# Item stage of a recommendation kernel: part of the gathered neighbours read by ScalarE, VectorE and SyncE instead of GpSimd

## The chip, the cores and the metric

The kernel runs on one core of a Trainium2 chip. The metric is device microseconds (us) of one execution. The time before is 36,303.63 us, the median of three runs that lie between 36,298.54 and 36,312.89 us. The profile is one further execution, and its own time is given below beside its span.

Engine names follow the profile: PE is TensorE, DVE is VectorE, ACT is ScalarE, POOL is GpSimd, SP is SyncE. PEld is the loading of weights into PE. SPq, ACTq and POOLq are the queues in which those engines issue DMAs.

## The reference

Every item has a row of 32 numbers in each of two tables, `E_in` and `E_out`, and a list of 32 neighbour items. For every item and both tables the reference takes a softmax attention over the item's neighbours; the result is used for 16,384 users with 100 history items each.

```
def _neighbor_attn(E, near_full):                  # twice: E_in and E_out, 50001 x 32
    V = E[near_full]                               # 50001 x 32 neighbours x 32
    scores = einsum('nd,nkd->nk', E, V) / sqrt(32)
    w = softmax(scores, axis=-1)
    return einsum('nk,nkd->nd', w, V)
...
h = concat([E_hist[history], a_sus[history], a_inf[history]])   # 16384 x 100 x 128
t = concat([E_tgt[target], a_inf[target], a_sus[target]])       # 16384 x 128
x = h * t[:, None, :]
z = relu(x @ W1.T + b1)
scores = z @ W2[0]                                 # then a masked exponential weighting, and a
...                                                # cosine and sigmoid for each user
```

All values are float32. The item numbers are random, so neighbour rows lie anywhere in the tables.

## The kernel before

The work has two stages, one after the other. They meet in two tables in DRAM, `table` and `ttab`, which the first stage writes and the second gathers from.

**The item stage** (lines 94 to 164) goes over 50,048 items (`ROWS`, the items with padding) in 23 iterations of 17 tiles (`NITER`, `NSUB`). A tile is 128 items, one on each partition; there are 391. `egeo` in DRAM holds both tables side by side, so one item's row is 64 floats, 256 bytes. At the start of an iteration SP loads the neighbour numbers `nidx`, the items' own rows `own`, and 64 columns of `row`. Then, for each tile:

- POOL gathers: 32 indirect DMAs (line 111), each of which fetches for all 128 items the row of their k-th neighbour into `v`, a tile of 128 x 32 x 64. `v` has five buffers, so POOL can be five tiles ahead of the arithmetic.
- ACT copies the items' own rows into PSUM (line 118).
- DVE multiplies all neighbours with the own row (`prod`, line 120), sums to scores (`sc`, line 127), takes the maximum and scales it (`top`, lines 129 and 130).
- ACT takes the exponentials with their sum (`ex`, `tot`, line 134).
- DVE inverts the sum (line 142), weighs the neighbours (`wv`, line 145, one instruction for each of the two tables), sums (`att`, line 152) and writes into `row` (line 153).
- ACT copies two halves, exchanged, into `trow` (line 160).

After 17 tiles SP writes `row` and `trow` to the tables (lines 163 and 164). The pools and the framework's scheduler set the order on each engine; a tile's instructions all stand before the next tile's. PE does nothing in this stage.

**The user stage** (lines 166 to 276) is not touched. For 128 groups of 128 users it gathers 100 history rows each with POOL (line 233), turns them on PE, multiplies by the target row, and runs the two matrix products.

The `with` statement that opens the item stage's pools, and the loops inside it, are what the diff replaces.

Of the kernel before, what the change touches and what calls it, by code (L numbers as in the profile page):

```python
# [9 lines left out]

F32 = mybir.dt.float32
I32 = mybir.dt.int32
AF = mybir.ActivationFunctionType
ALU = mybir.AluOpType
AX = mybir.AxisListType

P = 128
ITEMS = 50001
K = 32
G = 32  # L20
DE = 64
D = 128
# [7 lines left out]
NSUB = 17  # L30
NITER = -(-ITEMS // (P * NSUB))
ROWS = NITER * P * NSUB

# [7 lines left out]
def kernel(  # L43
# [11 lines left out]
    out: bass.AP,  # L55
):
    nc = tc.nc

    const = ctx.enter_context(tc.tile_pool(name="const", bufs=1))
    dram = ctx.enter_context(tc.tile_pool(name="dram", bufs=1, space=bass.MemoryType.DRAM))  # L60


    table = dram.tile([ROWS, D], F32, name="table")

    ttab = dram.tile([ROWS, D], F32, name="ttab")

    ident = const.tile([P, P], F32, name="ident")
# [16 lines left out]
    scale = 1.0 / math.sqrt(G)  # L84
    near_v = near.rearrange("(i p j) k -> i p j k", p=P, j=NSUB)
    egeo_v = egeo.rearrange("(i p j) d -> i p j d", p=P, j=NSUB)
    ehist_v = ehist.rearrange("(i p j) d -> i p j d", p=P, j=NSUB)
    table_v = table.rearrange("(i p j) d -> i p j d", p=P, j=NSUB)
    ttab_v = ttab.rearrange("(i p j) d -> i p j d", p=P, j=NSUB)

    nc.scalar.dma_start(ttab[0 : ITEMS - 1, 0:DE], etgt[0 : ITEMS - 1, :])
    nc.scalar.dma_start(ttab[ITEMS - 1 : ITEMS, 0:DE], etgt[ITEMS - 1 : ITEMS, :])
    with (
        tc.tile_pool(name="n_in", bufs=2) as n_in,
        tc.tile_pool(name="n_v", bufs=5) as n_v,
        tc.tile_pool(name="n_p", bufs=2) as n_p,
        tc.tile_pool(name="n_s", bufs=3) as n_s,
        tc.tile_pool(name="n_ps", bufs=2, space=bass.MemoryType.PSUM) as n_ps,
    ):
        for it in range(NITER):  # L100
            nidx = n_in.tile([P, NSUB, K], I32, name="nidx")
            nc.sync.dma_start(nidx, near_v[it])
            own = n_in.tile([P, NSUB, 2 * G], F32, name="own")
            nc.sync.dma_start(own, egeo_v[it])
            row = n_in.tile([P, NSUB, D], F32, name="row")
            nc.sync.dma_start(row[:, :, 0:DE], ehist_v[it])
            trow = n_in.tile([P, NSUB, 2 * G], F32, name="trow")
            for j in range(NSUB):
                v = n_v.tile([P, K, 2, G], F32, name="v")
                for k in range(K):  # L110
                    nc.gpsimd.indirect_dma_start(  # L111
                        out=v[:, k].rearrange("p t d -> p (t d)"),
                        out_offset=None,
                        in_=egeo,
                        in_offset=bass.IndirectOffsetOnAxis(ap=nidx[:, j, k : k + 1], axis=0),
                    )
                own_ps = n_ps.tile([P, 1, 2 * G], F32, name="own_ps")
                nc.scalar.copy(own_ps[:, 0, :], own[:, j, :])  # L118
                prod = n_p.tile([P, K, 2, G], F32, name="prod")
                nc.vector.tensor_tensor(  # L120
                    prod.rearrange("p k t d -> p k (t d)"),
                    v.rearrange("p k t d -> p k (t d)"),
                    own_ps.to_broadcast([P, K, 2 * G]),
                    ALU.mult,
                )
                sc = n_s.tile([P, 2, K], F32, name="sc")
                nc.vector.tensor_reduce(sc.rearrange("p t k -> p k t"), prod, AX.X, ALU.add)  # L127
                top = n_s.tile([P, 2], F32, name="top")
                nc.vector.tensor_reduce(top, sc, AX.X, ALU.max)
                nc.vector.tensor_scalar(top, top, -scale, None, ALU.mult)  # L130
                ex = n_ps.tile([P, 2, K], F32, name="ex")
                tot = n_s.tile([P, 2, 1], F32, name="tot")
                for t in range(2):
                    nc.scalar.activation(  # L134
                        ex[:, t, :],
                        sc[:, t, :],
                        AF.Exp,
                        bias=top[:, t : t + 1],
                        scale=scale,
                        accum_out=tot[:, t, :],  # L140
                    )
                nc.vector.reciprocal(tot, tot)  # L142
                wv = n_p.tile([P, 2, G, K], F32, name="wv")
                for t in range(2):
                    nc.vector.tensor_tensor(  # L145
                        wv[:, t].rearrange("p d k -> p k d"),
                        v[:, :, t, :],
                        ex[:, t, :].rearrange("p (k o) -> p k o", o=1).to_broadcast([P, K, G]),
                        ALU.mult,
                    )  # L150
                att = n_s.tile([P, 2, G], F32, name="att")
                nc.vector.tensor_reduce(att, wv, AX.X, ALU.add)  # L152
                nc.vector.tensor_tensor(  # L153
                    row[:, j, DE:D].rearrange("p (t d) -> p t d", t=2),
                    att,
                    tot.to_broadcast([P, 2, G]),
                    ALU.mult,
                )
                for t in range(2):
                    nc.scalar.copy(  # L160
                        trow[:, j, t * G : (t + 1) * G], row[:, j, D - (t + 1) * G : D - t * G]
                    )
            nc.sync.dma_start(table_v[it], row)
            nc.sync.dma_start(ttab_v[it][:, :, DE:D], trow)


    num = const.tile([P, UC], F32, name="num")
# [3 lines left out]
    hist_v = history.rearrange("(p i j) l -> i p j l", p=P, j=BSUB)  # L171
    tidx = const.tile([P, UC], I32, name="tidx")
    nc.scalar.dma_start(tidx, target.rearrange("(p c) -> p c", p=P))
    tidf = const.tile([P, UC], F32, name="tidf")
    nc.vector.tensor_copy(tidf, tidx)
    with (
# [12 lines left out]
        def target_rows(c):  # L189

            if c % BSUB == 0:
                hidx = u_in.tile([P, BSUB, L], I32, name="hidx")
                nc.sync.dma_start(hidx, hist_v[c // BSUB])
# [11 lines left out]
        def target_work(c):  # L205
# [8 lines left out]
            junk = u_t.tile([P, D], F32, name="junk")  # L214
            nc.scalar.activation(junk, t, AF.Square, accum_out=tsq[:, c : c + 1])
            idf = u_s.tile([P, L], F32, name="idf")
# [11 lines left out]
        def gather(c, g):  # L228
            u = users[c]
            h = u_h.tile([P, LG, D], F32, name="h")  # L230
            for q in range(LG):
                l = g * LG + q
                nc.gpsimd.indirect_dma_start(  # L233
                    out=h[:, q, :],
                    out_offset=None,
                    in_=table,
                    in_offset=bass.IndirectOffsetOnAxis(ap=u["hidx"][:, l : l + 1], axis=0),
                )
            u["h", g] = h

        def turn(c, g):
            u = users[c]
            h = u.pop(("h", g))
            hT_ps = ps_t.tile([P, LG, P], F32, name="hT_ps")
            for q in range(LG):
                nc.tensor.transpose(hT_ps[:, q, :], h[:, q, :], ident)  # L246
            xT = u_x.tile([D, LG, P], F32, name="xT")
            nc.vector.tensor_tensor(xT, hT_ps, u["tT"].to_broadcast([D, LG, P]), ALU.mult)  # L248
            nc.vector.tensor_reduce(u["hsum"][:, g * LG : (g + 1) * LG], h, AX.X, ALU.add)  # L249
            u["xT"][g] = xT  # L250

        def hidden(c, g):
# [3 lines left out]
            z = u_x.tile([HID, LG, P], F32, name="z")  # L256
            nc.scalar.activation(z, z_ps, AF.Relu, bias=b1_sb)  # L257
            u["z"][g] = z

        def scored(c, g):  # L260
# [9 lines left out]
            ea = u_s.tile([P, L], F32, name="ea")  # L270
            nc.scalar.activation(ea, u["score"], AF.Exp)
            nc.vector.tensor_tensor(ea, ea, u["keep"], ALU.mult)
# [7 lines left out]
        for s in range(len(groups) + 2):  # L280
            if s < len(groups):
                c, g = groups[s]
# [12 lines left out]
    with (  # L295
# [3 lines left out]
        root = f_s.tile([P, UC], F32, name="root")  # L299
        nc.scalar.activation(root, den, AF.Sqrt)  # L300
        part = f_s.tile([P, UC], F32, name="part")
# [6 lines left out]
        s = f_s.tile([P, 1], F32, name="s")  # L308
# [4 lines left out]
        nc.vector.tensor_scalar(n1, n1, float(D), EPS * EPS, ALU.mult, ALU.max)  # L313
        nc.scalar.activation(n1, n1, AF.Sqrt)
        n2 = f_s.tile([P, UC], F32, name="n2")
# [65 lines left out]
```

## Time and profile before

| | |
|---|---|
| median of three runs | 36,303.63 us |
| the profiled execution, whole | 31,810.23 us |
| its span, first to last instruction | 31,808.5 us |
| first and last gather issue of the item stage (line 111) | 9.7 and 15,626.3 us |
| first gather issue of the user stage (line 197) | 15,649.06 us |
| HBM read and written | 1,308.76 MB and 51.30 MB |
| SP's DMAs in the whole kernel | 151 |

The profiled execution is 14% shorter than the runs that were timed. Durations and stage times are from the profile, and they are compared with the span. The page gives busy time by engine, the span in 40 slices, the DMA queues, the chain of work that ended last, and the costliest groups of instructions. In a group's row, the busy time and the mean duration of one instruction stand after the first bar, and after the second the idle time of the engine just before such instructions, with what ended it. "issue" there means that the engine waited for nothing that the profile shows.

### The profile page before, as it was taken

Reading aid. Unit: us, or ns where it says so; the run is one execution under the profiler, and the core shown is the slowest. Engines: PE = TensorE matmul, PEld = TensorE weight load, DVE = VectorE, ACT = ScalarE, POOL = GpSimd, SP = SyncE. Lnnn points to the kernel's source line nnn. Section 1 sums busy time; section 2 is a strip of 40 time slices with the busy share of each in tenths; the row PEclk is TensorE's granted clock in tenths of the full one; section 3 lists DMA queues with packets and bytes.
Section 4 is the critical chain, followed back from the end, with each engine's and each line's share of the span. In section 5 each row is a group of like instructions: output and inputs, shape, how many; then the busy total and the mean of one; then the engine's idle time right before and its main releaser. Section 6 shows DMA issues by size and latency. Waiting matters only on the chain.

```text
span 31808.5 us, 154035 instructions
## 1 busy us (share of the span) xinstructions
PE 15238.9 (48%) x44931; PEld 9632.2 (30%) x44931; DVE 8951.2 (28%) x10957; ACT 2851.2 (9%) x6458; POOL 24005.7 (75%) x25446
## 2 busy tenths in 40 slices
PE   0000000000000000000299999999999999999999
PEld 0000000000000000000155555555555555555555
DVE  2222222222222222222222222222222222222222
ACT  0000000000000000000011111111111111111111
POOL 7777777777777777777777777777777777777777
PEclk9999999999999999999955555555555555555555
DMA  2111111111111111111122222222222222222221
GB/s 50 30 30 30 30 31 33 30 30 30 30 34 30 30 30 30 31 33 28 37 54 53 54 53 54 53 54 54 53 54 53 54 53 54 54 53 54 53 54 52
DMA packets 981064, 1358.75 MB, mean 43 GB/s; under 512 B 559872, under 2 KB 564352, under 8 KB 977280
## 3 DMA queue, kind: packets, MB, share of 16 engines
q0 software_dynamic: 814080, 1258.87, 17.1%
q1 hardware_dynamic: 115952, 77.16, 0.9%
q10 hardware_dynamic: 50192, 12.87, 0.2%
q8 instruction: 363, 5.95, 0.1%
q14 instruction: 477, 3.91, 0.0%
HBM read 1308.76 MB, written 51.30 MB: 43 GB/s over the span
## 4 chain that ended last, share of the span: by engine, by line
POOL 49%; issue 19%; PE 15%; DMA 14%; DVE 2%; ACT 1%; POOLq 0%; ACTq 0%; SPq 0%; DVEq 0%
POOL v L111 35%; POOL h L233 13%; DMA h<-table,hidx 11%; PE z_ps L255 7%; PE score L265 5%; PE hT_ps L246 3%; DMA v<-in_egeo_dram,nidx 2%; DVE xT L248 2%; ACT z L257 1%; POOL t L197 0%; POOLq L233 0%; DVE tT L211 0%; DVE ea L274 0%; DMA nidx<-in_near_dram 0%; DMA ttab<-trow 0%
## 5 line engine op out<-in xcount | busy, mean ns | idle before, releaser
L233 POOL DMA_INDIRECT h<-table,hidx x12800 | 12079.2, 944 | 3900.9 <-issue 3159.2
L111 POOL DMA_INDIRECT v<-in_egeo_dram,nidx x12512 | 11805.1, 943 | 3820.9 <-issue 3719.2
L209 PE MATMUL hT_ps<-ident,t 128*128 128x128 f32 x128 | 53.9, 421 | 15644.7 <-DMA t<-ttab,tidx 15644.7
L265 PEld LDWEIGHTS score<-w_sb,z 128*128 128x128 f32 x25600 | 6225.7, 334 | 1080.8 <-ACT z L257 1074.0
L255 PE MATMUL z_ps<-xT,w1T 128*128 128x512 f32 x6400 | 6526.7, 1123 | 0.0
L265 PE MATMUL score<-w_sb,z 128*128 128x1 f32 x25600 | 5903.9, 335 | 235.4 <-ACT z L257 150.2
L246 PE MATMUL hT_ps<-ident,h 128*128 128x128 f32 x12800 | 4715.0, 439 | 673.3 <-DMA h<-table,hidx 520.3
L249 DVE TENSOR_REDUCE hsum<-h 128x4 f32<-128x512 f32 x3200 | 2194.7, 686 | 9243.7 <-DMA h<-table,hidx 9226.9
L209 PEld LDWEIGHTS hT_ps<-ident,t 128*128 128x128 f32 x128 | 28.8, 225 | 15644.9 <-ACT idf L217 15644.9
L246 PEld LDWEIGHTS hT_ps<-ident,h 128*128 128x128 f32 x12800 | 2676.6, 209 | 5434.3 <-issue 3257.2
L120 DVE TENSOR_TENSOR prod<-v,own_ps 128x2048 f32<-128x2048 f32 x391 | 894.6, 2288 | 10794.7 <-DMA v<-in_egeo_dram,nidx 10794.4
L257 ACT ACTIVATE z<-z_ps,b_sb 128x512 f32<-128x512 f32 x3200 | 2199.1, 687 | 13448.3 <-PE z_ps L255 13335.1
L248 DVE TENSOR_TENSOR xT<-hT_ps,tT 128x512 f32<-128x512 f32 x3200 | 2210.2, 691 | 2028.6 <-PE hT_ps L246 2026.8
L255 PEld LDWEIGHTS z_ps<-xT,w1T 128*128 128x128 f32 x6400 | 1745.4, 332 | 0.0
L145 DVE TENSOR_TENSOR wv<-v,ex 128x1024 f32<-128x1024 f32 x782 | 1398.8, 1867 | 0.0
L118 ACT COPY own_ps<-own 128x64 f32<-128x64 f32 x391 | 84.4, 216 | 11499.9 <-DVE prod L120 11498.4
L127 DVE TENSOR_REDUCE sc<-prod 128x64 f32<-128x2048 f32 x391 | 894.5, 2288 | 13.4
L152 DVE TENSOR_REDUCE att<-wv 128x64 f32<-128x2048 f32 x391 | 893.8, 2286 | 13.4
L160 ACT COPY trow<-row 128x32 f32<-128x32 f32 x782 | 131.7, 215 | 2465.7 <-DVE row L153 2465.7
L134 ACT ACTIVATE ex<-sc,top 128x32 f32<-128x32 f32 x782 | 227.7, 291 | 1081.9 <-DVE top L130 1069.2
L142 DVE RECIPROCAL tot<-tot 128x2 f32<-128x2 f32 x391 | 64.8, 166 | 362.3 <-ACT ex L134 362.3
L197 POOL DMA_INDIRECT t<-ttab,tidx x128 | 120.7, 943 | 60.5 <-issue 60.5
(49 smaller groups left out, 808.6 us busy)
## 6 DMA issues: line engine op xcount, KB each, us to landing
h<-table,hidx POOLq DMA_INDIRECT x12800, 2.5
v<-in_egeo_dram,nidx POOLq DMA_INDIRECT x12512, 2.4
table<-row SPq DMA_DIRECT2D x23, 1088.0 KB, 4.4
own<-in_egeo_dram SPq DMA_DIRECT2D x23, 544.0 KB, 3.6
row<-in_ehist_dram SPq DMA_DIRECT2D x23, 544.0 KB, 6.7
ttab<-trow SPq DMA_DIRECT2D x23, 544.0 KB, 6.8
ttab<-in_etgt_dram ACTq DMA_DIRECT2D x1, 12500.0 KB, 53.5
hidx<-in_history_dram SPq DMA_DIRECT2D x32, 200.0 KB, 2.5
```

Of the source, the lines that this page charges most:

```text
L111: nc.gpsimd.indirect_dma_start(out=v[:, k].rearrange("p t d -> p (t d)"), out_offset=None, in_=egeo, in_offset=bass.IndirectOffsetOnAxis(a ...
L120: nc.vector.tensor_tensor(prod.rearrange("p k t d -> p k (t d)"), v.rearrange("p k t d -> p k (t d)"), own_ps.to_broadcast([P, K, 2 * G]), ...
L127: nc.vector.tensor_reduce(sc.rearrange("p t k -> p k t"), prod, AX.X, ALU.add)
L145: nc.vector.tensor_tensor(wv[:, t].rearrange("p d k -> p k d"), v[:, :, t, :], ex[:, t, :].rearrange("p (k o) -> p k o", o=1).to_broadcast ...
L152: nc.vector.tensor_reduce(att, wv, AX.X, ALU.add)
L233: nc.gpsimd.indirect_dma_start(out=h[:, q, :], out_offset=None, in_=table, in_offset=bass.IndirectOffsetOnAxis(ap=u["hidx"][:, l : l + 1], ...
L246: nc.tensor.transpose(hT_ps[:, q, :], h[:, q, :], ident)
L248: nc.vector.tensor_tensor(xT, hT_ps, u["tT"].to_broadcast([D, LG, P]), ALU.mult)
L249: nc.vector.tensor_reduce(u["hsum"][:, g * LG : (g + 1) * LG], h, AX.X, ALU.add)
L255: nc.tensor.matmul(z_ps, w1T, u["xT"].pop(g), start=True, stop=True)
L257: nc.scalar.activation(z, z_ps, AF.Relu, bias=b1_sb)
L265: nc.tensor.matmul(u["score"][:, l : l + 1], z[:, q, :], w2_sb, start=True, stop=True)
```

## The change

The change is in the item stage alone.

1. **A transposed table in SBUF.** `geoT` is a tensor of 128 partitions by 25,024 floats (100,096 bytes a partition). Column c holds the rows of items 2c and 2c+1: 64 floats of the even item on partitions 0 to 63, 64 of the odd one on the rest. It is built once, before the first tile's arithmetic, in 66 blocks (`transposed`): SP loads a block of 384 pairs (two staging buffers), PE transposes it in three instructions, ACT copies the result from PSUM.
2. **The last 3 of the 32 neighbours** (`NAUX`) no longer come by DMA. For each of 128 items one engine copies one column of `geoT`, four bytes on each of 128 partitions, into a tile `g`. The column's address is a value in a register, and one instruction loads 32 such values from SBUF (`registers`). A block is one load and 32 copies; of the twelve blocks of a tile ACT has seven and DVE five (`AUX`). PE then transposes the three `g` tiles back (`turn`), ACT copies the even halves into `v` (`even`), and DVE overwrites with the odd halves where the item number is odd (`odd_half`, a predicated copy).
3. **The 29th neighbour** is, in two tiles of three (`SPNUM`, `SPDEN`), fetched by SP: four register loads and 128 DMAs of 256 bytes each, at addresses in registers. In the third tile POOL fetches it as before.
4. **Register values.** At an iteration's load DVE computes the addresses in seven small instructions, PE transposes them, DVE copies them to `cols`. The next iteration's load now stands in the middle of an iteration.
5. **Order.** PE, ACT, DVE and SP run in the order in which the code stands; POOL is left to the scheduler. In step s the columns of tile s are cut into blocks among the products, scores and exponents of tile s-1, the weighting of tile s-2, and the closing copies of tile s-3. The pools of `prod` and `wv` go from two buffers to one.
6. The writes of `row` and `trow` go from SP's queue to ACT's.

POOL's issues in this stage go from 12,512 to 11,078. ACT gets 2,737 register loads and 87,584 column copies, DVE 1,955 and 62,560, SP 1,044 and 33,408 DMAs.

```diff
+AUX = ("AAAA", "AAAD", "DDDD",)
+NAUX = len(AUX)
+SPNUM, SPDEN = 2, 3
+NREG = 32
+PAIRS = ROWS // 2
+NST = 3
...
+    geoT = nc.alloc_sbuf_tensor("geoT", (P, PAIRS), F32).ap()
+    geoT_at = nc.sbuf_base - 4 * PAIRS
+    geoT_b = geoT.bitcast(U8)
...
+        tc.manual_schedule(engines={E.PE, E.Activation, E.DVE, E.SP}),
+        tc.tile_pool(name="n_st", bufs=2) as n_st,
...
-        tc.tile_pool(name="n_p", bufs=2) as n_p,
+        tc.tile_pool(name="n_p", bufs=1) as n_p,
+        tc.tile_pool(name="n_g", bufs=2) as n_g,
...
+        def transposed(q):
+            h = min(P, (PAIRS - q * NST * P))
+            n = NST if h == P else 1
+            st = n_st.tile([P, NST, 4 * G], F32, name="st")
...
+                for r in range(m):
+                    nc.tensor.transpose(ps[:, r, 0:h], st[0:h, n0 + r, :], ident[0:h, 0:h])
...
+                    nc.scalar.copy(into[:, n0 : n0 + m, :], ps[:, 0:m, 0:h])
...
+        def registers(s, a, engine, i0, low, top):
+            it, j = divmod(s, NSUB)
+            r = j * (NAUX + 1) + a
+            _, vals = nc.values_load_multi_w_load_instructions(
+                its[it][5][r : r + 1, i0 : i0 + NREG],
...
+        def gather(s):
...
+            by_sp = s * SPNUM % SPDEN < SPNUM
+            if by_sp:
+                for i0 in range(0, P, NREG):
+                    vals = registers(s, 0, E.SP, i0, 0, (ITEMS - 1) * 8 * G)
+                    for i in range(NREG):
+                        nc.sync.dma_start(
+                            v[i0 + i : i0 + i + 1, k1].rearrange("p t d -> p (t d)").bitcast(U8),
+                            egeo_b[:, ds(vals[i], 8 * G)],
+                        )
+            for k in range(k1 if by_sp else k1 + 1):
+                nc.gpsimd.indirect_dma_start(
...
+        def columns(s, a, i0):
+            e = AUX[a][i0 // NREG]
+            vals = registers(s, a + 1, ENGINE[e], i0, geoT_at, geoT_at + 4 * (PAIRS - 1))
+            g = subs[s]["g"][a].bitcast(U8)
+            copy = nc.scalar.copy if e == "A" else nc.vector.tensor_copy
+            for i in range(i0, i0 + NREG):
+                copy(g[:, 4 * i : 4 * i + 4], geoT_b[:, ds(vals[i - i0] - geoT_at, 4)])
...
+            work = [
+                lambda: one and turn(s - 1),
+                lambda: (two and weighted(s - 2, 0), one and even(s - 1)),
+                lambda: two and weighted(s - 2, 1),
+                lambda: one and (odd_half(s - 1), products(s - 1)),
+                lambda: one and scores(s - 1),
+                lambda: two and attend(s - 2),
+                lambda: three and finish(s - 3),
+                lambda: one and exponents(s - 1),
+            ]
+            for w in range(len(work)):
+                work[w]()
+                if s < NT:
+                    for blocks in (acts, dves):
+                        n = len(blocks)
+                        for c in blocks[-(-w * n // 8) : -(-(w + 1) * n // 8)]:
+                            columns(s, *c)
```

In the changed kernel the gathers of POOL stand at line 215, SP's 128 DMAs at line 210, the column copies at line 229 and the register loads at line 189.

## The prediction

> **What bounds the kernel now.** I read the page first, its busy table, slices and chain, then the two stages in windows, then one period in order of time, then the durations of single lines.
>
> The page, for one execution:
>
> ```profile
> span 31808.5 us, 154035 instructions
> PE 15238.9 (48%) x44931; PEld 9632.2 (30%) x44931; DVE 8951.2 (28%) x10957; ACT 2851.2 (9%) x6458; POOL 24005.7 (75%) x25446
> POOL 7777777777777777777777777777777777777777
> ...
> POOL 49%; issue 19%; PE 15%; DMA 14%; DVE 2%; ACT 1%; POOLq 0%; ACTq 0%; SPq 0%; DVEq 0%
> ...
> L111 POOL DMA_INDIRECT v<-in_egeo_dram,nidx x12512 | 11805.1, 943 | 3820.9 <-issue 3719.2
> ```
>
> POOL is level from end to end, and its idle time before line 111 is "issue": it waits for nothing. Two stages, busy time by engine (columns: window, length, PE, PEld, DVE, ACT, POOL, clock, DMA share, GB/s):
>
> ```profile
> 20.00:15600.00 15580.00, 0.00 (x0) 0.00 (x0) 4349.21 (x3511) 539.60 (x2730) 11776.44 (x12482) 1.00 0.16 31
> 15700.00:31700.00 16000.00, 15104.47 (x44545) 9548.94 (x44546) 4544.63 (x7358) 2282.68 (x3675) 12094.37 (x12817) 0.51 0.21 53
> ```
>
> The item stage is half the span, and there DVE is busy 28%, ACT 3%, PE never. One issue takes 15580/12482 = 1.248 us. A tile of 128 items has 32 issues, so 39.94 us; 391 tiles make 15,617 us. One tile in order of time:
>
> ```profile
> 7999.79 2.29 DVE L120 TENSOR_TENSOR prod<-v,own_ps 128x2048 f32<-128x2048 f32 x1 [27.67 <-DMA v<-in_egeo_dram,nidx]
> ...
> 8005.78 0.17 DVE L142 RECIPROCAL tot<-tot 128x2 f32<-128x2 f32 x1 [0.93 <-ACT ex L134]
> 8005.86 3.58 DVE L145 TENSOR_TENSOR wv<-v,ex 128x1024 f32<-128x1024 f32 x2
> ...
> 8012.06 0.34 ACT L160 COPY trow<-row 128x32 f32<-128x32 f32 x2 [6.30 <-DVE row L153]
> ...
> 8039.86 2.29 DVE L120 TENSOR_TENSOR prod<-v,own_ps 128x2048 f32<-128x2048 f32 x1 [27.84 <-DMA v<-in_egeo_dram,nidx]
> ```
>
> VectorE waits 28 us of each 40 for the gathered rows. These lines also price small operations. A Reciprocal of two elements holds VectorE 0.08 us before the next starts, though it is recorded as 0.17. Two copies of 32 elements take ScalarE 0.34 us while one is recorded as 0.215, so they start 0.125 apart.
>
> SyncE, which gets most new instructions, is idle but for 151 DMAs. Their issues at the start, and the spread for three lines (minimum, median, maximum ns):
>
> ```profile
> 1.19 0.42 SPq L74 DMA_DIRECT2D w_sb<-in_w_dram  x1
> 1.66 0.50 SPq L76 DMA_DIRECT2D w_sb<-in_w_dram  x1
> 2.20 0.44 SPq L102 DMA_DIRECT2D nidx<-in_near_dram  x1
> 2.68 0.44 SPq L104 DMA_DIRECT2D own<-in_egeo_dram  x1
> ```
>
> ```profile
> L163 SPq DMA_DIRECT2D table<-row x23: 326/326/332, 702.4 to 15641.0; - x23
> L130 DVE TENSOR_SCALAR top<-top x391: 168/170/245, 60.7 to 15633.7; 128x2 f32<-128x2 f32 x196
> L111 POOL DMA_INDIRECT v<-in_egeo_dram,nidx x12512: 940/944/1097, 9.7 to 15626.3; - x199
> ```
>
> One alone costs SyncE 0.33 us; in a row they start 0.44 to 0.54 apart.
>
> **What the Trainium skill says.** Perfetto Trace Analysis, Optimizing Scalar/DVE Operations, gives a fixed busy cost of about 60 ns to a VectorE instruction on SBUF and 93 ns to one of ScalarE, with recorded durations about twice that. The trace agrees: 82 ns, and 125 ns less 28 elements at 0.83 ns (the rate in ScalarE: Activation LUTs, What ACT_TABLE_LOAD costs), about 101 ns for four elements. SBUF - State Buffer, Who interferes with whom, says that a VectorE copy inside SBUF can take the port pair that GpSimd shares, and the later one blocks. The trace has one such operation a tile, L130: its 168 ns grow to 245 at most, and line 111's median stays 944.
>
> **The change part by part.**
>
> *GpSimd.* Per tile 32 issues become 29, and 28 in two tiles of three: 28.33 on average, 11,078 in all, 1,434 fewer. 1,434 x 1.248 = 1,790 us off the stage, 35.36 us a tile. Nothing else on the path is removed. What is late next is whichever other engine needs over 35.36 us for its new share.
>
> *ScalarE.* It gets 7 blocks a tile: one register load of 32 values and 32 copies of four bytes each. Copies: 224 x 0.101 = 22.6 us. A register load appears nowhere in the trace. DMA: Bandwidth & Descriptors, Latency and other measured facts, has a floor of about 600 ns for it; Runtime: NRT & Kernel Launch, Instruction fetch mechanics, has 200 ns a register from HBM, which would be 6.4 us for 32. These lie in SBUF, so I take 0.6: 4.2 us. The rest is 1.7 us (own 0.22, exponents 0.89, two trow copies 0.24, the new even copy of 192 elements about 0.3). Sum 28.5 us: hidden under 35.36.
>
> *VectorE.* Old work is 11.3 us (8012.03 - 7999.79 less the 0.93 waited). It gets 5 blocks: 160 x 0.082 = 13.1, loads 3.0, the predicated copy about 0.4, the index arithmetic of seven small operations per 17 tiles 0.1. Sum 27.9 us: hidden too. The port costs 75 ns at most per GpSimd issue, 28 x 0.075 = 2.1 us; still hidden. The other way round, GpSimd delayed by a running copy, is bounded by 0 and 0.08 us an issue, 0 to 890 us in all; I take 0, since line 111 shows no lengthening.
>
> *SyncE.* Each served tile needs 128 DMAs of 256 bytes at loaded addresses and 4 register loads; two tiles in three make 85.3 DMAs and 2.67 loads a tile. The nearest rows are 0.33 alone and 0.48 in a row, both for 128 rows of a tile; with some 45 ns between two, the low end is 0.375. One row has less to describe, but an address to fetch; I take 0.40. Then 85.3 x 0.40 + 2.67 x 0.6 = 35.7 us a tile, range 33.6 to 42.6. So SyncE stands level with GpSimd, and a hair sets it ahead: **the pace is 35.7 us**.
>
> *Waits.* The product of a tile (on VectorE) now also waits for SyncE's rows and ScalarE's even copy. Queued behind it are three column blocks of the next tile, for which TensorE's turn waits, and behind that the release of v. v has five buffers and is freed two tiles later, so GpSimd has over two periods of room. In a steady state the engines run side by side and the slowest sets the pace.
>
> *Start.* 66 loads, 196 transposes and 66 ScalarE copies build the transposed table before any column can be read. SyncE reaches them after the row load, which in the trace of before goes out at 54.2 us. With two staging buffers each takes about (2.5 landing + 0.5 issue + 1.2 transposes)/2 = 2.1 us, 137 us together, up to 191. SyncE's first rows end at 191 + 51 = 242 and the first v is free at about 270. GpSimd has filled its five tiles at 10 + 142 x 1.248 = 187 and waits some 85 us; I take 90, range 40 to 130. The end of the stage gets a few us longer at most.
>
> *Sum on the profiled execution:* 391 x (39.94 - 35.7) = 1,658, less 90 = 1,568 us off. The user stage is untouched. The execution takes 31,810 us with its surroundings, the median of the runs is 36,304, 14.1% more, and no view says where the 4,493 us lie. If evenly, the gain grows with it and gives 36,304 x 30,242/31,810 = 34,515. If in the user stage, it stays: 34,736. Between them: **34,600**.
>
> **Rivals.**
> 1. *SyncE sets the pace and eats part of the gain.* At 0.43 us a DMA a tile takes 38.3 us: 391 x 1.64 - 90 = 551 off, **35,750**. For: the row at the start, 0.44 and more. Against: single issues at 0.33, and these are small.
> 2. *SyncE makes it slower.* Break-even is where its tile reaches 39.94 - 90/391 = 39.71 us, a DMA of 0.447 us. At 0.48 it takes 42.6 us: 391 x 2.66 + 90 = 1,130 more, **37,430**. GpSimd then fills five tiles and waits for SyncE's row in each.
> 3. *ScalarE's queue makes it slower.* Its break-even is a copy of 0.150 us, or a register load of 2.2 us. If copies at a register address don't overlap, 224 x 0.188 + 5.9 = 48.0 us a tile: 391 x 8.06 + 90 = 3,240 more, **39,540**; at 6.4 us a load, 69 us a tile. Against: two neighbouring copies overlap in the trace. For: none there has an address from a register.
> 4. *GpSimd is held up by 160 VectorE copies a tile.* At the bound of 0.08 us an issue, 28.33 x 1.328 = 37.6 us, 826 off, **35,480**.
>
> **How the numbers follow.** Forecast 0.57, own range 34,100 (all of the unexplained 4,493 us in the item stage: 0.359 us on each of 12,512 issues, 1,434 x 1.607 = 2,305 less 90) to 35,300 (0.42 us a DMA). Rivals 1 and 4 together 0.17. A draw among them 0.04. Rival 2 0.10, rival 3 0.12. A measurement of this kernel tells about 0.2% from no change, 73 us. Faster 0.74, same 0.04, slower 0.22. Forecast, 1, 4 and the draw hold 0.78; the upper end goes a little into rival 2: 34,100 to 36,900.
>
> **What would show it.** Right: the item stage ends near 14,100 us in the profile; line 215's issues 1.25 us apart, with short waits for v at tile ends; SyncE's issues nearly gapless, at 0.40; ScalarE and VectorE at 75 to 80% of the period; ScalarE's copies 0.10 apart. Rival 2: SyncE gapless at over 0.45 and GpSimd idle for v. Rival 3: VectorE waiting for the even copy or the exponents, copies 0.15 apart or loads over 2 us. Wrong altogether: line 215's median well over 944, or a user stage other than 16,160 us.

## The result, and the profile after

The changed kernel takes 44,221.26 us, the median of four runs (44,216.16 to 44,229.2), beside 36,301.08 us for the kernel before: 1.218 times as long, interval 1.216 to 1.220. The forecast was 34,600.

The page of the changed kernel, the parts that answer to those shown of the kernel before:

```profile
span 44227.4 us, 386169 instructions
PE 14967.6 (34%) x46323; PEld 9744.9 (22%) x46323; DVE 14449.9 (33%) x74069; ACT 12531.1 (28%) x94499; POOL 22649.6 (51%) x24012
POOL 4344444444444444444444366666666666666666
...
PE 18%; another core or an unknown queue 14%; issue 5%; ACT 4%; DVE 1%; ACTq 0%; DMA 0%; POOL 0%; DVEq 0%; POOLq 0%
...
L215 POOL DMA_INDIRECT v<-in_egeo_dram,nidx x11078 | 10453.3, 944 | 14859.5 <-DVE v L247 11465.3
```

GpSimd is no longer level: in the item stage it is busy four tenths. One gather still lasts 944 ns, but before the gathers GpSimd stands idle for 14,859 us, 11,465 of them put down to VectorE (line 247, the predicated copy of the odd halves), which is not yet done with a `v`. The bound has gone from GpSimd to whatever holds up the others. (The shares of the chain add up to 42%: the page follows it back through the user stage only.) The two stages in windows (window, length, PE, PEld, DVE, ACT, POOL, clock, DMA share, GB/s):

```profile
20.00:25300.00 25280.00, 511.70 (x1380) 219.01 (x1380) 10037.45 (x66052) 10135.95 (x89939) 10434.49 (x11059) 1.00 0.08 19
25500.00:44100.00 18600.00, 14334.15 (x44579) 9448.61 (x44580) 4279.95 (x7365) 2283.45 (x3679) 12122.08 (x12851) 0.52 0.16 46
```

The item stage lasts 25,300 us, and **no engine is busy for even 42% of it**. That is the riddle of this case. The second surprise is the user stage, 18,700 us from its first history gather to its last, where the first profile of the kernel before had 16,140, though nothing in it changed. So the kernel before was profiled once more (experiment e1), and this second page differs from the first:

```profile
span 36137.5 us, 154035 instructions
...
L111 POOL DMA_INDIRECT v<-in_egeo_dram,nidx x12512 | 13387.4, 1070 | 4106.0 <-issue 3995.1
```

Its item stage ends at 17,494 us (first profile: 15,627) and its user stage takes 18,548. The first profile showed an execution 12% shorter than the runs that were timed (they are 14% longer than it); this one has about their length. Against it the stages compare as follows:

| | before, second profile | changed |
|---|---|---|
| item stage, last gather | 17,494 us | 25,313 us |
| per tile, on average | 44.7 us | 64.7 us |
| user stage, first to last history gather | 18,548 us | 18,700 us |

Of the 8,090 us between the two spans 7,820 lie in the item stage. What happens there is seen in stretches of 10 us, six of them being about one tile (columns as above):

```profile
10010.00:10020.00 10.00, 0.69 (x2) 0.28 (x2) 6.07 (x46) 7.34 (x70) 0.00 (x0) 1.00 0.01 1
10020.00:10030.00 10.00, 0.00 (x0) 0.00 (x0) 6.99 (x36) 5.91 (x56) 6.81 (x8) 1.00 0.09 21
10030.00:10040.00 10.00, 0.00 (x0) 0.00 (x0) 2.37 (x11) 1.74 (x9) 7.56 (x9) 1.00 0.12 26
10040.00:10050.00 10.00, 0.00 (x0) 0.00 (x0) 1.34 (x7) 1.35 (x7) 7.56 (x9) 1.00 0.12 26
10050.00:10060.00 10.00, 0.00 (x0) 0.00 (x0) 1.51 (x7) 1.35 (x7) 5.42 (x6) 1.00 0.10 23
10060.00:10070.00 10.00, 0.47 (x1) 0.18 (x1) 5.85 (x45) 6.30 (x63) 0.00 (x0) 1.00 0.01 1
```

GpSimd works in bursts of 28 or 29 gathers (the last of the five busy columns). Some microseconds into a burst ScalarE falls from 70 instructions in 10 us to 7, VectorE from 46 to 7, and both come back after the burst ends. The engines take turns. Within the burst, in order of time:

```profile
10040.33 3.50 SPq L210 DMA_DIRECT2D v<-in_egeo_dram  x2
10041.02 0.94 POOL L215 DMA_INDIRECT v<-in_egeo_dram,nidx  x1 [0.30 <-issue]
10041.05 0.19 ACT L229 COPY g<-geoT 128x4 uint8 x1 [1.21 <-issue]
10041.05 0.17 DVE L229 COPY g<-geoT 128x4 uint8 x1 [1.20 <-issue]
10042.27 0.94 POOL L215 DMA_INDIRECT v<-in_egeo_dram,nidx  x1 [0.30 <-issue]
10042.45 0.19 ACT L229 COPY g<-geoT 128x4 uint8 x1 [1.21 <-issue]
10042.45 0.17 DVE L229 COPY g<-geoT 128x4 uint8 x1 [1.23 <-issue]
```

Each copy lasts what it always lasts, 0.17 and 0.19 us, but the next starts 1.40 us later, and the wait is "issue": nothing in the program asks for it. ScalarE and VectorE start at the same moment. Nothing depends on anything here, and yet three engines move in step.

### The profile page after: what moved, and what is told of

Same layout as the page of the kernel before. It is cut to its first block, busy times and chain, and to the rows that moved or that the text cites. A ratio compares the mean times of both kernels' runs of the same rounds, so it can differ in the third digit from the quotient of the medians.

```text
span 44227.4 us, 386169 instructions
## 1 busy us (share of the span) xinstructions
PE 14967.6 (34%) x46323; PEld 9744.9 (22%) x46323; DVE 14449.9 (33%) x74069; ACT 12531.1 (28%) x94499; POOL 22649.6 (51%) x24012
## 5 line engine op out<-in xcount | busy, mean ns | idle before, releaser
L215 POOL DMA_INDIRECT v<-in_egeo_dram,nidx x11078 | 10453.3, 944 | 14859.5 <-DVE v L247 11465.3
L229 ACT COPY g<-geoT 128x4 uint8 x87584 | 9671.5, 189 | 14919.8 <-issue 13658.1
L229 DVE COPY g<-geoT 128x4 uint8 x62560 | 5708.7, 175 | 10977.6 <-issue 10735.9
L234 PE MATMUL pt<-ident,g 128*128 128x128 f32 x1173 | 455.8, 456 | 23456.8 <-ACT g L229 23071.7
L460 PEld LDWEIGHTS score<-w_sb,z 128*128 128x128 f32 x25600 | 5958.7, 328 | 5344.7 <-ACT z L452 4072.2
L234 PEld LDWEIGHTS pt<-ident,g 128*128 128x128 f32 x1173 | 184.9, 196 | 23720.7 <-ACT g L229 23329.4
L441 PE MATMUL hT_ps<-ident,h 128*128 128x128 f32 x12800 | 4131.4, 426 | 5.9 <-DMA h<-table,hidx 5.1
L441 PEld LDWEIGHTS hT_ps<-ident,h 128*128 128x128 f32 x12800 | 3309.2, 263 | 3612.9 <-issue 3561.2
```

The costliest lines, as they stand in the source:

```text
L215: nc.gpsimd.indirect_dma_start(out=v[:, k].rearrange("p t d -> p (t d)"), out_offset=None, in_=egeo, in_offset=bass.IndirectOffsetOnAxis(a ...
L229: copy(g[:, 4 * i : 4 * i + 4], geoT_b[:, ds(vals[i - i0] - geoT_at, 4)])
L460: nc.tensor.matmul(u["score"][:, l : l + 1], z[:, q, :], w2_sb, start=True, stop=True)
```

## The experiments

All ratios are to the kernel before, run beside each experiment on the same chip. In the expectations of e2 and e3, A is the theory that SyncE's DMAs set the pace and B that the columns do; from e4 on A is the starvation that the stretches above show.

**e1, the kernel before unchanged.**

> The kernel before, unchanged, for a second profile. If the 4,493 us between its profiled execution and its timed runs lie in the user stage, this run takes 36,300 us with an item stage that ends near 15,650 us and a user stage of 20,600 us. If they lie in GpSimd's issues, an issue takes 1.42 us and the item stage ends near 17,800 us. If the first profile was typical of profiles, the span is 31,800 us again.

36,144.78 us, ratio 1.0002 (0.9992 to 1.0012). Its profile is the second one shown above.

**e2 and e3, each half of the change alone.** e2 leaves SyncE's rows out (GpSimd gathers them), e3 leaves the columns, the transposed table and the merging out.

```
-SPNUM, SPDEN = 2, 3
+SPNUM, SPDEN = 0, 3                                       # e2
...
-            for k in range(k1 if by_sp else k1 + 1):
+            for k in [k for k in range(K) if not (by_sp and k == k1)]:   # e3
-                            columns(s, *c)
```

> SyncE's rows go back to GpSimd (29 issues in every tile); the columns on ScalarE and VectorE stay. Theory A, SyncE sets the pace of 61 us a tile because it is starved while GpSimd issues: the pace falls to GpSimd's 29 x 1.248 = 36.2 us and the item stage ends near 14,300 us. Theory B, the columns set it (register loads of 2 us, cross waits of ScalarE, VectorE and TensorE): the pace stays near 60 us and the item stage ends near 24,000 us.

> SyncE's rows stay, the columns go: GpSimd gathers the last three neighbours (31.3 issues a tile), no transposed table is built. Theory A: still some 60 to 65 us a tile, with SyncE slow during GpSimd's bursts; item stage about 24,000 us. Theory B: GpSimd's 31.3 x 1.248 = 39.1 us a tile or SyncE's own 85.3 x 0.32 + 2.67 x 2.1 = 33 us, so about 15,300 us.

e2: 42,090.33 us, ratio 1.1645 (1.1611 to 1.1679), item stage to 23,356 us. e3: 43,782.19, ratio 1.2113 (1.2078 to 1.2148), item stage to 24,984. The columns alone bring 5,949 us, three quarters of the loss, SyncE's rows alone 7,641, nearly the whole of it, and the two together little more. Two independent costs would have added up. Neither theory in its first form survives: the halves have in common that they put many small instructions beside the gathers.

**e4, e7 and e5, instructions without their purpose.** These are the kernel before with copies from a constant tile into a scratch tile. They have no register, no load and nothing that reads what they write. In the program e4 has 384 small ones per tile, e7 has 96, and e5 has 17 wide ones. The scheduler, which orders these engines in the kernel before, does not keep them so: in the traces e7's copies all lie in the first 7,784 us, and a quarter of e5's copies on ScalarE fall into the user stage.

```
+                for x in range(224):                       # 56 in e7
+                    nc.scalar.copy(outa[:, x : x + 1], src[:, x : x + 1])
+                for x in range(160):                       # 40 in e7
+                    nc.vector.tensor_copy(outd[:, x : x + 1], src[:, x : x + 1])
                 own_ps = n_ps.tile([P, 1, 2 * G], F32, name="own_ps")
...
+                for x in range(11):                        # e5; 6 on VectorE
+                    nc.scalar.copy(outa[:, 0:2048], src[:, 0:2048])
```

> The kernel before, with 224 copies of one column (128x1) on ScalarE and 160 on VectorE added per tile, at constant addresses, from a constant tile into a scratch tile that nobody reads: the instruction count of the changed kernel's columns without its loads, loaded addresses, transposes and waits. Theory A (while GpSimd issues gathers, the other engines get only about one instruction per 0.7 us between them once some 15 us of a burst have passed, so the NUMBER of their instructions costs time): the item stage grows from 17,500 to 22,000 to 25,000 us, the whole to 40,600 to 43,600. Rival B (the columns cost through their loads, addresses and the waits between engines): 224 x 0.095 = 21.3 us on ScalarE and 160 x 0.07 = 11.2 + 11.3 us on VectorE fit beside 44.8 us of GpSimd, and the time stays at 36,100 to 36,600.

> The kernel before with a quarter of the small copies, 56 on ScalarE and 40 on VectorE per tile. Theory A: the cost is there from the first instructions, since GpSimd's own gathers are already stretched in the kernel before: a quarter of the cost of 384, 37,000 to 38,500 us. If instead 96 instructions find room in the first 15 us of a burst: 36,100 to 36,500. Rival B: no change, 36,100 to 36,300.

> The kernel before, with 11 copies of 128x2048 on ScalarE and 6 on VectorE added per tile, from a constant tile into a scratch tile that nobody reads: about the busy time of the 384 small copies in 17 instructions. Theory A (the number of instructions costs, not their busy time): 17 more instructions beside 54 per tile, 36,100 to 37,500 us, far under the kernel with 384 small ones. Rival C (busy engines or their memory traffic hold up the gathers or each other): as slow as with the 384 small copies, over 40,000 us.

e4: 41,831.22 us, ratio 1.1572 (1.1539 to 1.1606). e7: 37,360.01, ratio 1.0335 (1.0305 to 1.0365). e5: 36,405.21, ratio 1.0071 (1.0048 to 1.0094). Copies that nobody needs cost about as much as the columns alone (5,686 us beside e2's 5,949), and their number decides, not their busy time. In the item stage e5's wide copies keep ScalarE busy for 6,117 us and VectorE for 2,855, e7's small ones 2,532 and 1,469. Yet e5's last gather is issued at 17,510 us, as in e1 (17,494), and e7's at 18,720. e5's 260 us more are not in its item stage.

Spread over both engines, one small copy costs (37,360 - 36,145)/(391 x 96) = 0.032 us in e7 and 5,686/(391 x 384) = 0.038 in e4. In e7 that is no test of a thinner spread: the tiles with copies hold some 270 each and take 53.5 us, those without 44.1. The end of a burst in e4, in order of time:

```profile
10042.71 0.94 POOL L115 DMA_INDIRECT v<-in_egeo_dram,nidx  x1 [0.30 <-issue]
10043.18 0.19 ACT L122 COPY outa<-src 128x1 f32<-128x1 f32 x1 [1.21 <-issue]
10043.90 0.15 DVE L124 COPY outd<-src 128x1 f32<-128x1 f32 x1 [1.25 <-issue]
10043.95 0.94 POOL L115 DMA_INDIRECT v<-in_egeo_dram,nidx  x1 [0.30 <-issue]
...
10049.49 0.19 ACT L122 COPY outa<-src 128x1 f32<-128x1 f32 x1 [0.52 <-issue]
10050.18 3.16 ACT L122 COPY outa<-src 128x1 f32<-128x1 f32 x33 [0.50 <-issue]
10050.19 5.78 DVE L124 COPY outd<-src 128x1 f32<-128x1 f32 x94 [0.54 <-issue]
```

One copy in 0.70 to 1.40 us on each engine while GpSimd issues. Some 5 us after the end of its last gather ScalarE runs 33 copies in 3.16 us, 0.096 each. The starts lie on one grid of 0.70 us for both engines (43.18, 43.90, ... 49.49, 50.18).

**e6, the changed kernel with GpSimd nearly idle.** Four gathers of seven neighbouring rows (eight in the last, where SyncE fetches none) in place of 28 or 29 single ones. As many bytes arrive; other neighbours are read, so its results are not those of the reference.

```
-            for k in range(k1 if by_sp else k1 + 1):
+            for k in (0, 7, 14, 21):
+                n = 7 if k < 21 or by_sp else 8
...
+                    in_=egeo[0 : n * 4096, :].rearrange("(c x) d -> c (x d)", x=n),
```

> The changed kernel with 4 gathers per tile on GpSimd in place of 28 or 29, each of 7 (or 8) rows that lie side by side, so that as many bytes arrive; which neighbours are read is changed, all other instructions stay. Theory A: with GpSimd nearly idle the other engines run at their own pace, ScalarE and VectorE about 31 us per tile, and the item stage takes 12,000 to 14,500 us, the whole 30,700 to 33,200. Rival B (the new order of loads, copies, transposes and waits takes its 62 us per tile by itself): item stage over 20,000 us, the whole over 38,500.

32,965.82 us, ratio 0.912 (0.9093 to 0.9146); the item stage ends at 14,213 us. All the loads, copies, transposes, SyncE DMAs and waits of the change are there, and a typical tile takes 31.3 us (the median distance between two tiles' exponentials), half of the changed kernel's 61.4. The new instruction order costs nothing like the loss. What costs is its company with the gathers. The engines take turns also by this sum: 28.33 gathers at 1.249 us are 35.4, and 31.3 for the others make 66.7, 5 us over what a tile of the changed kernel takes.

**e8 and e14, one column in place of three; e10 and e16, fewer instructions; e9.** e8 and e14 are one program, e10 and e16 another. e9 is e6 with 24 gathers of 16 rows added.

```
-AUX = ("AAAA", "AAAD", "DDDD",)
-SPNUM, SPDEN = 2, 3
+AUX = ("AAAD",)
+SPNUM, SPDEN = 0, 3
```

> The changed kernel with one neighbour per tile read as columns in place of three, and none by SyncE: 96 copies on ScalarE and 32 on VectorE per tile, 31 gathers on GpSimd. Theory A, with the price that the small copies had in the kernel before (0.032 to 0.038 us per instruction and tile): 128 copies, 4 loads and some 10 waits and transposes are 142 x 0.035 = 5.0 us more per tile, one gather of 1.40 less: 391 x 3.6 = 1,400 us more and 90 for the start: 37,300 to 38,000 us. If only the third column is too much and few instructions find room: 391 x 1.4 = 550 us less, 35,600 to 35,900.

31,327.67 us, ratio **0.9848** (0.9828 to 0.9868): the kernel before took 31,812.43 us beside it. This was another chip, and there everything is different. The page of e8:

```profile
POOL 7777777777777777777777777777777777777777
...
POOL 47%; issue 19%; PE 17%; DMA 13%; DVE 2%; ACT 1%; another core or an unknown queue 0%; POOLq 0%; ACTq 0%; SPq 0%; DVEq 0%
...
L215 POOL DMA_INDIRECT v<-in_egeo_dram,nidx x12121 | 11437.3, 944 | 3703.3 <-issue 3606.8
...
h<-table,hidx POOLq DMA_INDIRECT x12800, 2.5
```

GpSimd is level again, waits for nothing, and the gathers come 1.2485 us apart on average, beside 128 column copies a tile. The price of the prediction is confirmed here: 391 gathers fewer x 1.2485 = 488 us, measured 485. The last line, from the page's list of DMA issues, ends with the microseconds to landing, as the first profile of the kernel before does. In the page of the changed kernel the row stops before that:

```profile
h<-table,hidx POOLq DMA_INDIRECT x12800
```

Every profile of these experiments from a chip on which the kernel before took 36,130 us or more lacks these times, and all three from the chip with 31,812 have them. The same program on a chip where the kernel before took 36,295.53:

> The kernel of e8, one column per tile. Where the kernel before takes about 31,812 us: 31,327, as in e8. Where it takes about 36,200, theory A with 0.032 to 0.038 us for each of some 142 more instructions and one gather less: 37,300 to 38,000; if few instructions find room at no cost there: 35,600 to 35,900.

37,923.35 us, ratio **1.0449** (1.0419 to 1.0479). Its gathers in the page:

```profile
L215 POOL DMA_INDIRECT v<-in_egeo_dram,nidx x12121 | 11463.9, 946 | 7618.6 <-DVE wv L294 3956.1
```

So one program is 1.5% faster than the kernel before on one chip and 4.5% slower on another. In the item stage GpSimd's wait for VectorE tells the pages apart. Ten microseconds of e8 and of e14, in the columns of the stretches above:

```profile
5010.00:5020.00 10.00, 0.00 (x0) 0.00 (x0) 7.98 (x37) 6.99 (x69) 7.56 (x9) 1.00 0.15 27
5010.00:5020.00 10.00, 0.00 (x0) 0.00 (x0) 5.28 (x7) 1.27 (x7) 6.83 (x8) 1.00 0.14 26
```

Beside nine gathers ScalarE runs 69 instructions in e8, beside eight it runs 7 in e14. The price fits too: 37,923 - 36,296 + 391 x 1.40 = 2,175 us for 391 x 142 instructions (128 copies, and about 14 loads, waits and transposes), 0.039 each.

> The kernel of e6 (4 gathers of 7 rows side by side) with 24 more gathers per tile on GpSimd of 16 rows of 256 bytes each, into a tile that nobody reads: as many issues as in the changed kernel, with an eighth of its rows in these 24. Neighbours are read as in e6. If GpSimd's issues starve the others: about the changed kernel's time, 42,000 to 44,500 us. If it is the rows (the descriptors and their packets): nearer to e6, 33,000 to 36,500; the issues alone need 28 x 1.25 = 35 us per tile, 13,700 us for the stage, which is under e6's 14,210.

35,301.92 us, on the chip of e8. There it says nothing on the question that it was made for, whether GpSimd's issues starve the others or the rows that they fetch; this stays open. It also has a hold-up at each turn of an iteration, the reason of which is not known, so its time is no clean measure. But one stretch of 100 us is worth showing:

```profile
9700.00:9800.00 100.00, 3.96 (x10) 1.59 (x10) 75.54 (x545) 76.15 (x760) 73.47 (x88) 1.00 0.06 15
```

GpSimd issues 88 gathers, and beside it ScalarE runs 760 instructions and VectorE 545, about the pace of a typical tile of e6. On this chip the engines do run side by side, with all of the changed kernel's instructions on the others, though 24 of the 28 gathers of a tile fetch 16 rows only.

e10 and e16 let one set of VectorE and ScalarE instructions work on two tiles of the kernel before, with three buffers of `v` for two tiles each in place of five for one.

```
+            for j in range(0, NSUB, 2):
+                w = min(2, NSUB - j)
+                v = n_v.tile([P, 2, K, 2, G], F32, name="v")
...
+                nc.scalar.activation(ex[:, 0:w], dif[:, 0:w], AF.Exp, scale=scale)
```

> The kernel before with two tiles of items worked on by one set of VectorE and ScalarE instructions (the largest score is subtracted on VectorE, one exponential for both tiles and halves, the sums on VectorE), so that these engines have 14 instructions for two tiles in place of 32; GpSimd's gathers are the same. Theory A: fewer instructions beside the gathers. At 0.035 us each, 9 to 13 fewer per tile give 120 to 180 us, 35,950 to 36,030; if the stretch of the gathers, 4.8 us per tile, goes with the number of the others' instructions: half of 391 x 4.8 = 940, 35,200. If the gathers stretch by themselves: no change, 36,140.

> The kernel of e10, two tiles worked on by one set of VectorE and ScalarE instructions. Where the kernel before takes about 31,812 us: no change, as in e10. Where it takes about 36,200, theory A: 9 to 13 instructions fewer per tile at 0.032 to 0.038 us give 110 to 190 us less; if the stretch of the gathers (4.8 us per tile) goes with the number of the others' instructions, up to 940 us less. If the gathers stretch by themselves: no change.

31,812.31 us, ratio 1.0000 (0.9991 to 1.0009), and on a chip of the other kind 36,134.73, ratio 0.9998 (0.9989 to 1.0007). A miss: the price of added instructions is not paid back when some are taken away. The gathers of e16 last 1,069 ns on average, as they do in e1, so GpSimd's gathers are stretched there by themselves. In e1, in order of time:

```profile
8031.15 0.96 POOL L111 DMA_INDIRECT v<-in_egeo_dram,nidx  x1 [0.31 <-issue]
8032.42 1.09 POOL L111 DMA_INDIRECT v<-in_egeo_dram,nidx  x1 [0.30 <-DMA v<-in_egeo_dram,nidx]
8033.82 1.10 POOL L111 DMA_INDIRECT v<-in_egeo_dram,nidx  x1 [0.30 <-issue]
8035.22 1.10 POOL L111 DMA_INDIRECT v<-in_egeo_dram,nidx  x1 [0.30 <-issue]
```

From 1.25 us apart they go to 1.40, twice the step of 0.70, with no other engine at work.

**e11, e13, e15, e17 and e18: the changed kernel again, for a chip of the second kind.** e12 is e4's program, run beside e11.

> The changed kernel as it is. Theory D: the starvation belongs to the execution, not to the kernel: it was there in every execution whose page gives no landing times for the gathers (the changed kernel and the first seven experiments), and absent where the page gives them (the first profile of the kernel before and the last three experiments). If this call's kernel before takes about 31,812 us: GpSimd issues its 28.33 gathers per tile every 1.2485 us, 35.4 us, above the 31.3 us in which the other engines did a tile beside a nearly idle GpSimd, so the item stage takes 391 x 35.4 = 13,840 us, 90 for the start, and up to 250 for the stall once in 17 tiles; with a user stage of 16,160 the whole is 30,000 to 30,500 us, ratio 0.943 to 0.959. If the kernel before takes about 36,140: 44,200 us as before. Rival E: the changed kernel is slow on its own, whatever the execution: over 36,000 us where the kernel before takes 31,812.

> The kernel before with 224 small copies on ScalarE and 160 on VectorE per tile once more. Theory D: if this call's kernel before takes about 31,812 us, the copies find room beside the gathers (21 us on ScalarE, 11 + 11 on VectorE, of 40 us per tile) and the time is 31,800 to 32,000; if it takes about 36,140, 41,830 as before. Rival E (the number of instructions costs in every execution): 35,000 us or more where the kernel before takes 31,812.

> The changed kernel as it is. Where the kernel before takes about 31,812 us. Theory D (the starvation belongs to the execution): 30,000 to 30,500 us, from 35.4 us of GpSimd per tile. Rival E (the changed kernel is slow on its own): over 36,000. Where the kernel before takes about 36,200: 44,200.

None of them was on such a chip. e11: 44,178.01 us, ratio 1.2176 (1.2156 to 1.2197). e12: 42,071.72, ratio 1.1597 (1.1574 to 1.162). e13: 44,184.66, e15 43,908.17, e17 44,298.7, e18 43,902.49, ratios 1.2148 to 1.2187, with expectations like e13's. Wherever the changed kernel ran, six times with the result, the loss is the same. **What the changed kernel takes where the kernel before takes 31,812 us was not measured.** That it would gain there rests on e8, where a third of the columns gained what its gather costs, and on the stretch of e9.

No version with the reference's results is faster than the kernel before on both kinds of chip.

## Why the prediction was wrong

1. *"1,434 x 1.248 = 1,790 us off the stage."* The price of a gather held: 944 ns in the changed kernel, 1.249 us from one to the next (median), and e8 returned it to 3 us. But it was taken from an execution of another kind than those that were timed. There the gathers of the kernel before come 1.3975 us apart.

2. *"What is late next is whichever other engine needs over 35.36 us for its new share"*, and *"In a steady state the engines run side by side and the slowest sets the pace."* **This step failed.** Measured with GpSimd nearly idle, the other engines' share takes 31.3 us in a typical tile (e6), under 35.36, so by the rule GpSimd should have stayed the bound. (SyncE's rows come to 33.8 on average. With the hold-up of point 8 the mean tile of e6 takes 36.2, hardly more.) Instead a tile takes 61.4 us, because in these executions the others hardly get an instruction in while gathers are issued: the burst of 28 or 29 gathers, some 35 us, and the others' work stand behind one another. The condition that the rule rests on, that engines don't share anything, was never asked of the trace. It couldn't be seen in the first profile, in which beside the gathers there ran only some 16 other instructions a tile.

3. *Register loads at 0.6 us.* The trace of the changed kernel, for one line each the durations in ns (minimum, median, maximum):

```profile
L189 ACTq TENSOR_LOAD <-cols x2737: 1938/1986/6072, 277.3 to 25421.1; - x196
L189 DVEq TENSOR_LOAD <-cols x1955: 2097/2152/2360, 58.1 to 25416.8; - x196
```

```profile
L210 SPq MOVE v<-in_egeo_dram x33408: 2/29/1423, 277.7 to 25397.4; - x199
L210 SPq DMA_DIRECT2D v<-in_egeo_dram x33408: 2/225/1504, 277.8 to 25397.5; - x199
```

A load of 32 values takes 2.0 to 2.2 us. Put in whole, it would add 7 x 1.39 = 9.7 us a tile on ScalarE and carry the prediction's own sum of 28.5 over 35.36. It doesn't count whole: the load starts while the copies before it are still being done. ScalarE in e6, three blocks in a row:

```profile
8011.03 3.21 ACT L231 COPY g<-geoT 128x4 uint8 x32 [0.93 <-issue]
8015.18 3.14 ACT L231 COPY g<-geoT 128x4 uint8 x32 [0.94 <-issue]
8019.26 3.14 ACT L231 COPY g<-geoT 128x4 uint8 x32 [0.94 <-issue]
```

ScalarE idles some 0.94 us before each, and the copies come 0.095 us apart, cheaper than put down. That is about 30 us in place of 28.5, still under 35.36, so this isn't what decided. The Trainium skill's floor of about 600 ns (DMA: Bandwidth & Descriptors, Latency and other measured facts) was no price for 32 values, and its 200 ns a register from HBM (Runtime: NRT & Kernel Launch, Instruction fetch mechanics) was three times too much for values in SBUF: 62 to 68 ns each.

4. *SyncE at 0.40 us a DMA, "level with GpSimd".* A DMA takes 225 ns and a register move before it 29, and the DMAs come 0.32 us apart. From first to last, a tile's 128 take 50.7 us in e6, loads between them included, where 128 x 0.40 + 4 x 0.6 = 53.6 were put down: this held. The maxima, 1.50 and 1.42 us, are the starved ones: even a register move waits for up to two steps of the grid. Rivals 1 and 2 made SyncE the cause; without SyncE's part the time is 42,090 us (e2), so it isn't the one cause. But an instruction more on SyncE costs more than one of e4's copies: in e3, with 261 gathers of 1.40 us fewer, (7,641 + 365)/67,860 = 0.118 us. The price of 0.032 to 0.039 holds for work spread over ScalarE and VectorE.

5. *Rival 3* named ScalarE's queue, with copies over 0.15 us apart or loads over 2 us as its signs. Both signs came: from the first gather of a burst to its last ScalarE's copies are 0.48 us apart on average, and VectorE's loads take 2.15. Its mechanism was wrong: e4 has neither loads nor loaded addresses, and loses about as much as e2.

6. *Rival 4*, GpSimd held up by VectorE's copies, is refuted: line 215's duration stays at 944 ns with 160 copies a tile. The Trainium skill (SBUF - State Buffer, Who interferes with whom) says that such copies can block GpSimd; no run here shows it.

7. *The 4,493 us "of which no view says where".* The second profile shows it: 1,867 us more in the item stage and 2,412 more in the user stage. So it was spread over both, as the forecast had it in part. But it is no constant share to scale by: in e1's item stage it comes from gathers stretched to 1.40 us, on the steps of 0.70 us that the starved stretches have. The prediction's own sign for "wrong altogether", a user stage other than 16,160 us, was there for the kernel before already.

8. *Not foreseen:* once in 17 tiles ScalarE's copies stand for some 49 to 65 us (once 104) until the write of `trow` to DRAM is done, 1,255 us in all, by the view of waits on line 229. In e8 no tile takes over 39.4 us, so there it doesn't show. It is some 3 us a tile, no part of the riddle: e2 has no tile over 65 us and loses three quarters.

## What to carry to other kernels

Where the timed runs are longer than the profiled execution by more than they differ from each other, profile again before pricing anything: the missing time may be the very limit that the change will meet. An engine that is idle has not for that reason room for instructions: put as many harmless ones beside the bound engine first, as e4 does, and see what they cost. Replacing one gather of 1.25 to 1.40 us by 128 small instructions pays only where each costs less than about 0.010 us, and on the chips of the first kind on which this was measured they cost 0.032 to 0.039 (e4, e7, e12, e14).

## What the runs showed of the hardware

- There are two kinds of execution of one program. On six chips the kernel before took 36,130 to 36,360 us, on one 31,812; the first profile is of the second kind too. One chip of the first kind was used twice and was so both times, so the kind goes with the chip as far as that shows. The one of the second kind was used once.
- In the first kind, while GpSimd issues indirect DMAs, instructions of SyncE, ScalarE and VectorE start on a common grid of 0.70 us, mostly one or two steps apart on each engine, down to register moves. In the burst of e4 shown above that sets in 6 us after the first gather, at first with a few copies at each step, and ends 5 us after the last. GpSimd keeps its 1.249 us there, and stretches to 1.40 in e1 and e16, where the others have little to do.
- There is an exception. After a register load within a burst VectorE runs eight or nine copies at its own pace before the grid returns (346 of the 375 loads well inside a burst of the changed kernel); ScalarE runs one. It isn't explained here. In the changed kernel, right after a load:

```profile
10039.19 0.67 DVE L229 COPY g<-geoT 128x4 uint8 x8 [2.14 <-issue]
10041.05 0.17 DVE L229 COPY g<-geoT 128x4 uint8 x1 [1.20 <-issue]
10042.45 0.17 DVE L229 COPY g<-geoT 128x4 uint8 x1 [1.23 <-issue]
```

- The cause is open. Those executions lack the landing times of the gathers: e1's trace has 87,621 landing records where the first profile of the same program has 409,500. So event records are lost in them, and each time given here comes from an execution with a record. That recording and instructions share a path would fit (a register move has nothing else to wait for); it is argued, not shown, since no time without a record is at hand. Instruction fetch fits less: the changed kernel's page has 24.72 MB in its two queues of kind instruction for 386,169 instructions, 64 bytes each, and the packets of one queue are 8 KB, 128 instructions, while in a burst nearly every single start is held up. Nor do packets take longer: in e8 and e14, which are one program, those of that queue take 442 and 451 ns in the first 14,000 us (medians).
